# Attention layer: the edge products become the stationary operand of the segment sums, and the denominators go through the output weights

## The chip, the cores and the metric

The kernel runs on one core of a Trainium2 chip. The metric is the device time of one execution in microseconds (us), and the median of several executions is compared. A run's trace holds every instruction of one profiled execution.

## The reference, cut to what matters

Four graph layers follow each other, each with a residual and a layer norm, on 6,250 nodes with 160 features and 100,000 edges sorted by destination. A node's features are 64 scalars and 32 three-vectors. The first layer (L0) is an attention layer, and the change is in it alone. In short:

```
m1 = cg_tp(scalars, vectors of src + dst, edge harmonics, radial weights)   # 96 scalars, 128 three-vectors
a  = exp(score(m1, head) - max over the edges of dst)                       # 4 heads
m2 = cg_tp(gated values of m1, edge harmonics, w2)                          # 96 scalars, 128 three-vectors
val = m2 @ (Ws_vlin, Wv_vlin)                                               # per head 16 scalars, 8 three-vectors
out[dst, head] = sum over edges of a * val / sum over edges of a
```

The value projection is linear, so the kernel sums a*m2 over the edges first and projects the sums per node. One edge's m2 has 480 numbers: three blocks of 128 (the x, y and z parts of the vectors) and one block of 96 scalars. A further column 480 of m2 is a constant 1, whose sum is the softmax denominator.

## The kernel before, in words

The loop of L0 is `edge_loop0`. It takes the edges in windows (`Window0`) of three chunks (`WC = 3`) of 128 edges; 784 chunks make `NW0 = 262` windows. A window owns 32 destination nodes (`WM = 32`), and with 4 heads that gives 128 pairs of head and node. The order of all instructions is written out by hand: in slot `s` of `for s in range(NW0 + 10)`, the windows that entered 1, 2, ... 10 slots ago (`x2` to `x9`, `at(10)`) each do one stage. Every engine runs its instructions in the order in which the slot lists them.

The stages, with the lines of their main instructions:
- `load` gathers the features of the sources (L722, POOL).
- `ends` (L1229) spreads the features of the 32 destinations over the edges by matmuls of 32 rows, `weights` (L1239) makes the radial weights by matmuls of 32 rows.
- `product1` makes m1 on VectorE and GpSimd.
- `turn` transposes one chunk of m1 (four blocks, L1288) and ScalarE copies it out (L1290). `linear` (L1296, L1298) projects it, six passes of 32 columns among them; `gated` and `score` follow.
- `spread`, `scores` (L1330), `exps` and `by_edge` (L1352) make the masked exponentials `p`: edges in the partitions, 128 pairs of head and node in the columns.
- `product2` makes m2 of the window.
- `sums` (L1359): one matmul per chunk with `p` as the stationary operand and the 481 columns of m2 as the moving one. The result `pa` has head and node in the partitions. After the third chunk ScalarE copies it to `a` (L1362).
- `channels`: four transposes of `a` (L1367, L1368) put the 480 channels in the partitions, in four blocks; two copies make `aT` (L1370, L1371).
- `outputs`: one matmul with the 96x64 weights `w["ls"]` (L1377), three with the 128x32 weights `w["lv"]` (L1379). The denominator is copied from column 480 of `a` (L1386), and four copies of 32x40, one per head, fill `row` (L1392 on VectorE, then L1390 three times on ScalarE).
- `write` sends `row` to a table in memory.

A matmul on f32 operands is two passes in the trace, a transpose one; each pass is a load of the stationary operand (LDWEIGHTS, "PEld") and a stream of the moving columns (MATMUL, "PE"). In PSUM the tiles of `ends`, `sums` and `outputs` share one buffer (name `m`, `bufs=1`), so each of them waits until the one before has been read. The transposes of `turn`, `scores`, `by_edge` and `channels` share two buffers (name `t`).

In every fourth slot `radial` loads the harmonics and radial inputs of four windows, and GpSimd multiplies them (L1416). Below, such a slot is called a radial slot.

After the four layers' loops, `Heads` reads the table of L0 and divides by the denominators. Edges that fall outside of their window are handled by a second loop over `Window0`; it does not run on these inputs (L1379 has 1,572 passes, six for each of 262 windows).

## Time and profile before

| | |
|---|---|
| median of 3 runs | 8015.94 us (8013.83 to 8018.99) |
| the profiled execution | 8008.86 us, span 8007.1 us |
| mean granted TensorE clock | 0.948 |
| L0 loop, first L1229 to last L1229 | 306.3 to 3251.0 us |
| L0 loop, 400 to 3250 us: busy PE, DVE, POOL, ACT | 2825, 2294, 2180, 1549 us of 2850 |
| layer 1 loop, 3570 to 5440 us: busy PE, DVE, POOL, ACT | 1870, 1383, 1425, 1084 us of 1870 |
| most slots of the L0 loop | 10.79 us |
| radial slots (every fourth) | 11.55 us |

A slot's length is the distance between successive L1323, of which there is one in each slot. "PEclk" is the clock that TensorE was granted, as a share of the full one; it is 1.0 or 0.5 at any moment, and what lies between is a mean over a stretch. The end of a matmul is modelled in the trace, so a busy PE isn't a PE at its peak: distances from start to start tell what a pass costs.

### The profile page before, as it was taken

How to read it: one execution, taken by the hardware profiler on the slowest of the kernel's cores; microseconds unless marked ns; L12 is line 12 of the kernel's file. 1: busy time of each engine (PE TensorE's matmuls, PEld its weight loads, DVE VectorE, ACT ScalarE, POOL GpSimd, SP SyncE). 2: the span in 40 equal slices, each digit the busy share in tenths (PEclk: the TensorE clock that was granted, in tenths of full speed). 3: DMA queues.
4: the chain of work that ended last, by engine and by line, in shares of the span. 5: the costliest groups of instructions: out<-in, count | busy, mean ns of one | idle time of the engine just before them, and what ended most of it. 6: DMA issues, size and time to landing. Idle time of an engine off the chain costs nothing. (4 is left out here: it accounts for less than half of the span.)

```text
span 8007.1 us, 150406 instructions
## 1 busy us (share of the span) xinstructions
PE 7328.2 (92%) x49240; PEld 5720.5 (71%) x49240; DVE 5391.7 (67%) x11871; ACT 3997.6 (50%) x12138; POOL 5269.2 (66%) x5412
## 2 busy tenths in 40 slices
PE   4899999999999999789999999997888887888887
PEld 2677877787878878569999999995555556555556
DVE  5488888878888788557777777775444446555557
ACT  1255555555555555345555555555555554333334
POOL 0377777777777777117777777772777770677771
PEclk9999999999999999669999999996899998999999
DMA  4344444433333333235565656555333335444446
GB/s 137 99 121 111 112 116 119 109 61 63 60 64 60 64 60 63 53 103 99 100 103 98 100 101 100 98 88 144 87 86 86 86 85 178 112 110 110 110 110 228
DMA packets 645090, 799.53 MB, mean 100 GB/s; under 512 B 185122, under 2 KB 512146, under 8 KB 636722
## 3 DMA queue, kind: packets, MB, share of 16 engines
q1 hardware_dynamic: 404818, 501.89, 22.3%
q0 software_dynamic: 238880, 283.36, 20.5%
q8 instruction: 402, 6.59, 0.4%
q14 instruction: 414, 3.39, 0.1%
q10 hardware_dynamic: 576, 4.30, 0.1%
HBM read 548.48 MB, written 240.64 MB: 99 GB/s over the span
## 5 line engine op out<-in xcount | busy, mean ns | idle before, releaser
L722 POOL DMA_INDIRECT f<-feat,r_src x2352 | 2536.4, 1078 | 969.7 <-issue 550.8
L1081 POOL DMA_INDIRECT tab<-o,scat x784 | 1350.4, 1722 | 433.5 <-ACT o L1080 301.5
L857 PE MATMUL pa<-pr,oy 128*128 128x321 f32 (+1 forms) x3136 | 1110.6, 492 | 0.0
L866 ACT COPY o<-pa 32x96 f32<-32x96 f32 (+4 forms) x2358 | 553.3, 245 | 843.4 <-PE pa L857 797.1
L1067 PE MATMUL pt<-same,tp 128*128 128x128 f32 x6272 | 895.5, 286 | 7.0 <-DVE tp L710 4.0
L857 PEld LDWEIGHTS pa<-pr,oy 128*128 128x128 f32 x3136 | 609.4, 199 | 371.0 <-issue 193.7
L1067 PEld LDWEIGHTS pt<-same,tp 128*128 128x128 f32 x6272 | 764.3, 192 | 24.2 <-PE pf L1051 16.3
L1290 ACT COPY xt<-t 128x512 f32<-128x512 f32 x784 | 460.8, 588 | 592.6 <-PE t L1288 568.7
L1359 PE MATMUL m<-m,p 128*128 128x481 f32 x1568 | 739.0, 581 | 0.9 <-ACT row L1390 0.9
L1069 ACT COPY xt<-pt 128x512 f32<-128x512 f32 x784 | 459.6, 586 | 524.3 <-PE pt L1067 524.3
L1298 PEld LDWEIGHTS z<-w_mv,xt 128*128 128x128 f32 x4704 | 622.1, 195 | 0.0
L1078 PE MATMUL po<-ov,xt 128*128 128x32 f32 x4704 | 611.6, 267 | 0.0
L1323 POOL COPY sc_all<-sc 128x384 f32<-128x384 f32 x262 | 302.8, 1156 | 464.2 <-DVE sc L1318 461.3
L1298 PE MATMUL z<-w_mv,xt 128*128 128x32 f32 x4704 | 601.5, 265 | 0.0
L1078 PEld LDWEIGHTS po<-ov,xt 128*128 128x128 f32 x4704 | 588.3, 192 | 0.0
L807 PE MATMUL ww<-w,hid 64*128 64x192 f32 (+1 forms) x2088 | 260.8, 364 | 297.1 <-DVE pr L839 170.7
L1288 PE MATMUL t<-ident,tp 128*128 128x128 f32 x3136 | 513.9, 288 | 0.0
L1288 PEld LDWEIGHTS t<-ident,tp 128*128 128x128 f32 x3136 | 385.3, 152 | 178.1 <-issue 126.1
L807 PEld LDWEIGHTS ww<-w,hid 64*128 64x128 f32 x2088 | 180.8, 189 | 443.9 <-ACT o L866 208.5
L1303 DVE SCALAR_TENSOR_TENSOR val<-th,z 128x96 f32<-128x96 f32 x784 | 196.3, 250 | 406.6 <-ACT la L1300 406.2
L846 DVE TENSOR_TENSOR pr<-f,ww 128x384 f32<-128x384 f32 x131 | 72.7, 555 | 561.8 <-DMA f<-feat,r_src 255.2
L1299 ACT ACTIVATE th<-z 128x96 f32<-128x96 f32 x784 | 197.0, 251 | 433.9 <-PE z L1298 396.3
(328 smaller groups left out, 16509.6 us busy)
## 6 DMA issues: line engine op xcount, KB each, us to landing
tab<-zeros SPq DMA_DIRECT2D x49, 1280.0 KB
nodes<-in_src_row_dram SPq DMA_DIRECT2D x98, 512.0 KB
dn<-in_dst_row_dram SPq DMA_DIRECT2D x261, 192.0 KB
f<-feat,r_src POOLq DMA_INDIRECT x2352
tb<-tab SPq DMA_DIRECT2D x24, 1280.0 KB
e<-in_ef64T_dram SPq DMA_DIRECT2D x196, 128.0 KB
dn<-in_dst_row_dram SPq DMA_DIRECT2D x196, 128.0 KB
e<-in_ef64T_dram SPq DMA_DIRECT2D x261, 96.0 KB
```

The costliest lines, as they stand in the source:

```text
L722: pool.indirect_dma_start(out=o, out_offset=None, in_=table, in_offset=bass.IndirectOffsetOnAxis(ap=idx, axis=0),)
L807: pe.matmul(self.ww[:, q, 0:wn], self.hid[k, c * P : (c + 1) * P], m, start=True, stop=True)
L857: pe.matmul(pa[:, 0:m], self.oy[:, q, :], self.pr[:, q, 0:m], start=c == 0, stop=c == self.ns[h] - 1)
L866: act.copy(o[q, at : at + e], pa[q, b0 * V : b0 * V + e])
L1067: pe.matmul(pt[:, k, :], self.tp[:, c, lo : lo + P], self.same[:, c, :], start=True, stop=True)
L1069: act.copy(self.xt, pt)
L1078: pe.matmul(po[:, 96 + i * V : 96 + (i + 1) * V], xt[:, 1 + i, :], w["ov"], start=True, stop=True)
L1081: pool.indirect_dma_start(out=self.tables[c % len(self.tables)], out_offset=bass.IndirectOffsetOnAxis(ap=self.scat[:, c : c + 1], axis=0), ...
L1288: pe.transpose(pt[:, k, :], self.tp[:, c, k * P : (k + 1) * P], ident)
L1290: act.copy(self.xt[c], pt)
L1298: pe.matmul(z[:, F + k * V : F + (k + 1) * V], xt[:, k, :], w["mv"], start=True, stop=True)
L1359: pe.matmul(self.pa, self.p[:, c * P : (c + 1) * P], self.m2[:, c, 0:481], start=c == 0, stop=c == self.n - 1)
```

## The change

- `sums` now goes by block `k` of channels. Each block of 128 columns of m2 is the stationary operand and `p` the moving one, so the result has the channels in the partitions and head and node in the columns. There are 12 matmuls of 128 columns in a window where there were three of 481.
- `channels` and its slot are gone, and so is the copy `a`. One copy of 128x512 from `pa` makes `aT`. `outputs` and `write` come one slot earlier (`x8` and `at(9)`), and the loop has one slot fewer.
- Column 480 of m2, the constant 1, is now row 96 of the fourth block of `aT`. The weights `ls` become 97 x 68: per head 16 columns and one more, whose only entry is a 1 in row 96. The matmul with `ls` thus gives the denominator of each pair as well. The copies into `row` take 41 columns, and the copy of the denominator is gone. In `row` and the table the denominator sits at column 16 of 41 instead of 40, and `Heads` reads it there.
- `ls` is set up by two memsets and a strided load.

```diff
-        def sums(self, c):
-            if c == 0:
-                self.pa = self.ps.tile([P, 481], F32, name="m", bufs=1)
-            pe.matmul(self.pa, self.p[:, c * P : (c + 1) * P], self.m2[:, c, 0:481], start=c == 0, stop=c == self.n - 1)
-            if c == self.n - 1:
-                self.a = self.sb.tile([P, 481], F32, name="a", bufs=4)
-                act.copy(self.a, self.pa)
-
-        def channels(self):
-            pt = self.ps.tile([P, 4, P], F32, name="t", bufs=2)
-            for k in range(3):
-                pe.transpose(pt[:, k, :], self.a[:, k * P : (k + 1) * P], ident)
-            pe.transpose(pt[0:96, 3, :], self.a[:, 384:480], ident)
-            self.at_ = self.sb.tile([P, 4, P], F32, name="aT", bufs=2)
-            act.copy(self.at_[:, 0:3, :], pt[:, 0:3, :])
-            act.copy(self.at_[0:96, 3, :], pt[0:96, 3, :])
+        def sums(self, k):
+            if k == 0:
+                self.pa = self.ps.tile([P, 4, P], F32, name="m", bufs=1)
+            q = slice(k * P, (k + 1) * P)
+            for c in range(self.n):
+                pe.matmul(
+                    self.pa[:, k, :], self.m2[:, c, q], self.p[:, c * P : (c + 1) * P], start=c == 0, stop=c == self.n - 1
+                )
+            if k == 3:
+                self.at_ = self.sb.tile([P, 4, P], F32, name="aT", bufs=2)
+                act.copy(self.at_, self.pa)
...
-            pe.matmul(o[:, :, 0:16], self.at_[0:96, 3, :], w["ls"].rearrange("k (h a) -> k h a", h=4), start=True, stop=True)
+            ls = w["ls"].rearrange("k (h a) -> k h a", h=4)
+            pe.matmul(o[:, :, 0:17], self.at_[0:97, 3, :], ls, start=True, stop=True)
...
-            vec.tensor_copy(row[:, 40:41], self.a[:, 480:481])
...
-                    act.copy(row[q, 0:40], o[q, h, :])
+                    act.copy(row[q, 0:41], o[q, h, :])
...
-                for s in range(NW0 + 10):
+                for s in range(NW0 + 9):
...
-                    chunk(x7, 0, "sums")
+                    sums(0)
                     chunk(x4, 1, "turn")
                     x5.exps()
-                    chunk(x7, 1, "sums")
-                    chunk(x7, 2, "sums")
+                    sums(1, 2, 3)
                     on(first, 3)
                     on(second, 3)
                     chunk(x4, 1, "linear", "gated")
                     chunk(x4, 2, "turn")
                     x6.by_edge()
                     x2.masks()
-                    x9.outputs()
+                    x8.outputs()
                     chunk(x4, 2, "linear")
-                    x8.channels()
                     chunk(x4, 2, "gated")
```

More of the change, by code (lines that the diff above doesn't have):

```diff
@@ L523, in begin @@
                 vec.tensor_add(t0[:, :, :, 0:41], t0[:, :, :, 0:41], t1[:, :, :, 0:41])
-                den = t0[:, :, :, 40]
+                den = t0[:, :, :, 16]
                 vec.tensor_scalar(den, den, 1e-16, None, ALU.add)
@@ L531, in begin @@
                 v_ = av[:, 0:m, S:F].rearrange("p j (h a) -> p h j a", h=4)
-                vec.tensor_mul(s_, t0[:, :, :, 0:16], bc(t0[:, :, :, 40], 3, 16))
-                vec.tensor_mul(v_, t0[:, :, :, 16:40], bc(t0[:, :, :, 40], 3, 24))
+                vec.tensor_mul(s_, t0[:, :, :, 0:16], bc(t0[:, :, :, 16], 3, 16))
+                vec.tensor_mul(v_, t0[:, :, :, 17:41], bc(t0[:, :, :, 16], 3, 24))
         def turn(self, i):
@@ L1354, in by_edge @@
             act.copy(self.p[:, 0:e], pt[:, 0:e])
-        def sums(self, c):
-            if c == 0:
-                self.pa = self.ps.tile([P, 481], F32, name="m", bufs=1)
-            pe.matmul(self.pa, self.p[:, c * P : (c + 1) * P], self.m2[:, c, 0:481], start=c == 0, stop=c == self.n - 1)
-            if c == self.n - 1:
-                self.a = self.sb.tile([P, 481], F32, name="a", bufs=4)
-                act.copy(self.a, self.pa)
-        def channels(self):
-            pt = self.ps.tile([P, 4, P], F32, name="t", bufs=2)
-            for k in range(3):
-                pe.transpose(pt[:, k, :], self.a[:, k * P : (k + 1) * P], ident)
-            pe.transpose(pt[0:96, 3, :], self.a[:, 384:480], ident)
-            self.at_ = self.sb.tile([P, 4, P], F32, name="aT", bufs=2)
-            act.copy(self.at_[:, 0:3, :], pt[:, 0:3, :])
-            act.copy(self.at_[0:96, 3, :], pt[0:96, 3, :])
+        def sums(self, k):
[9 more added lines that the diff above has]
+                act.copy(self.at_, self.pa)
         def outputs(self, old=None):
             w, row = self.w, self.row
-            po = self.ps.tile([P, F], F32, name="m", bufs=1)
-            o = po.rearrange("p (h q) -> p h q", q=40)
-            pe.matmul(o[:, :, 0:16], self.at_[0:96, 3, :], w["ls"].rearrange("k (h a) -> k h a", h=4), start=True, stop=True)
+            po = self.ps.tile([P, 4 * 41], F32, name="m", bufs=1)
+            o = po.rearrange("p (h q) -> p h q", q=41)
+            ls = w["ls"].rearrange("k (h a) -> k h a", h=4)
+            pe.matmul(o[:, :, 0:17], self.at_[0:97, 3, :], ls, start=True, stop=True)
             for k in range(3):
                 pe.matmul(
-                    o[:, :, 16 + 8 * k : 24 + 8 * k],
+                    o[:, :, 17 + 8 * k : 25 + 8 * k],
                     self.at_[:, k, :],
@@ L1389, in outputs @@
                 if h:
-                    act.copy(row[q, 0:40], o[q, h, :])
+                    act.copy(row[q, 0:41], o[q, h, :])
                 else:
-                    vec.tensor_copy(row[q, 0:40], o[q, h, :])
+                    vec.tensor_copy(row[q, 0:41], o[q, h, :])
             if old is not None:
@@ L1476, in edge_loop0 @@
                         ws.append(new)
-                    x2, x3, x4, x5, x6, x7, x8, x9 = (at(k) for k in range(2, 10))
+                    x2, x3, x4, x5, x6, x7, x8 = (at(k) for k in range(2, 9))
                     load, first, second = new.load(), x3.product1(), x5.product2()
@@ L1486, in chunk, with sums @@
                             getattr(x, name)(c)
-                    at(10).write(tabs[0][(s - 10) % tab_n[0]])
+                    def sums(*parts):
+                        for k in parts if x7.n else ():
+                            x7.sums(k)
+                    at(9).write(tabs[0][(s - 9) % tab_n[0]])
                     on(load)
@@ L1590, in edge_loop0 @@
                 x.by_edge()
-                for c in range(n):
-                    x.sums(c)
-                x.channels()
+                for k in range(4):
+                    x.sums(k)
                 x.outputs(old)
@@ L1677 @@
             act.copy(ms[:, 128:160], po[0:96, 0, 0:V])
-            ls = load(wp, t["L0_gnn_Ws_vlin"], 96, S, "w_ls")
+            ls = wp.tile([97, 4 * 17], F32, name="w_ls")
+            vec.memset(ls, 0.0)
+            vec.memset(ls[96:97, 16 : 4 * 17 : 17], 1.0)
+            l4 = ls[0:96, :].rearrange("k (h a) -> k h a", h=4)[:, :, 0:16]
+            nc.sync.dma_start(l4, t["L0_gnn_Ws_vlin"].rearrange("k (h a) -> k h a", h=4))
             lv = load(wp, t["L0_gnn_Wv_vlin"], P, V, "w_lv")
@@ L1693 @@
             vec.tensor_scalar(cv[96:P, :], cv[96:P, :], R2, None, ALU.mult)
-            vec.tensor_scalar(ls, ls, cs, 0.5, ALU.mult, ALU.mult)
+            vec.tensor_scalar(l4, l4, cs, 0.5, ALU.mult, ALU.mult)
             vec.tensor_scalar(lv, lv, cv, 0.5, ALU.mult, ALU.mult)
```

## The prediction

> **What bounds the kernel now.** The page's rows of busy time and of the 40 slices come first:

> ```profile
> PE 7328.2 (92%) x49240; PEld 5720.5 (71%) x49240; DVE 5391.7 (67%) x11871; ACT 3997.6 (50%) x12138; POOL 5269.2 (66%) x5412
> PE   4899999999999999789999999997888887888887
> PEclk9999999999999999669999999996899998999999
> ```

> Slices 2 to 15 are the attention loop. PE shows 9 there, no other engine does, and the clock is 9, not full. Two windows of busy time compare that loop with the one of layer 1 (columns after the stretch: busy us and instructions of PE, PEld, DVE, ACT, POOL, then the granted clock):

> ```profile
> 400.00:3250.00 2850.00, 2825.02 (x22778) 2279.61 (x22777) 2294.32 (x5314) 1548.81 (x4810) 2179.79 (x2838) 0.97 0.36 84
> 3570.00:5440.00 1870.00, 1869.60 (x15596) 1710.58 (x15596) 1382.53 (x2096) 1083.57 (x2402) 1425.03 (x866) 1.00 0.59 98
> ```

> TensorE bounds the attention loop: 99% busy, the next engine 80%. So I read its slot as a list of passes. The timeline of PE in a normal slot (start, modelled length, line, shape, passes):

> ```profile
> 571.17 0.60 PE L1288 MATMUL t<-ident,tp 128*128 128x128 f32 x4
> 571.60 1.78 PE L1359 MATMUL m<-m,p 128*128 128x481 f32 x4
> 573.22 0.44 PE L1296 MATMUL z<-w_ms,xt 96*128 96x160 f32 x2
> ...
> 574.88 0.33 PE L1377 MATMUL m<-w_ls,aT 96*128 96x64 f32 x2
> 575.05 0.81 PE L1379 MATMUL m<-w_lv,aT 128*128 128x32 f32 x6
> 575.69 0.52 PE L1296 MATMUL z<-w_ms,xt 96*128 96x160 f32 x2
> 576.05 0.75 PE L1298 MATMUL z<-w_mv,xt 128*128 128x32 f32 x6
> 576.64 0.53 PE L1367 MATMUL t<-ident,a 128*128 128x128 f32 x3
> 577.00 0.27 PE L1368 MATMUL t<-ident,a 128*96 128x128 f32 x1
> 577.20 1.08 PE L1229 MATMUL m<-fw,on 32*128 32x160 f32 x6
> 578.21 0.66 PE L1288 MATMUL t<-ident,tp 128*128 128x128 f32 x4
> ```

> Four passes of sums take 571.60 to 573.22, 0.404 us each. The transposes of `channels` take 576.64 to 577.20. The last view is the clock, by stretches of 3.4 us around one long slot:

> ```profile
> 596.60:600.00 3.40, 2.91 (x24) 2.71 (x24) 2.20 (x9) 2.85 (x12) 2.94 (x5) 1.00 0.20 51
> 600.00:603.40 3.40, 3.40 (x29) 2.74 (x31) 3.19 (x6) 1.55 (x5) 2.36 (x3) 0.50 0.65 64
> 603.40:606.80 3.40, 3.40 (x24) 3.07 (x18) 1.31 (x3) 0.35 (x2) 2.84 (x5) 0.50 0.13 33
> 606.80:610.20 3.40, 3.40 (x8) 1.80 (x8) 3.01 (x8) 0.99 (x2) 2.25 (x4) 0.50 0.09 24
> 610.20:613.60 3.40, 3.40 (x26) 2.78 (x24) 0.65 (x3) 1.89 (x6) 0.96 (x2) 1.00 0.13 30
> ```

> Between 600.0 and 610.2 us TensorE has half its clock, and the slot takes 15.65 us, not 10.79. From 400 us on, the loop has 24 such spells: 13 of 10.2 us, costing 4.86 us each, and 11 of 3.4 us, costing 1.58 us (12.37 for 10.79). Together 81 us.

> [...] every change of clock in this loop lies on one grid of 3.413 us. [...] the trace has 112 ns from load to load (below). [...]

> **The change part by part,** for a full-clock slot:
> - Sums, old: 6 passes x 0.404 = 2.42 us. New: 3 chunks x 4 blocks x 2 passes = 24 passes of 128 columns. Layer 1's L1067 has the same form, both operands in SBUF; eight loads take 0.97 us with the last one's 0.19 in it, so (0.97 - 0.19) / 7 = 0.112 us each:

> ```profile
> 3801.13 0.97 PEld L1067 LDWEIGHTS pt<-same,tp 128*128 128x128 f32 x8
> ```

>   24 x 0.1115 = 2.68 us, **+0.26 us**. Bounds: 0.109 us a pass (the transposes) gives +0.20; 0.114 gives +0.32.
> - `channels` goes: 577.20 - 576.64 = 0.56 us; the step to the 32-row matmuls, 0.206 us for 0.112, moves to the last L1298. **-0.47 us**.
> - `ends` (L1229) now follows the last L1298 directly. It needs PSUM buffer `m`, which the copies into `row` must have read. L1379 ends at 575.86; L1392 and the three L1390 end at 576.70; L1229 could stream at 576.74. Release and load put it at 576.8: a wait of 0 to 0.12 us, taken as **+0.05**. Behind it on PE stand the next `turn` and `weights`.
> - Sum: normal slot 10.79 - 0.16 = **10.63 us**. In radial slots L1377 stands idle about 0.65 us for the copy of the sums (ScalarE is late, behind VectorE, which L1416 slows). The longer sums run into that idle time, so only -0.47 + 0.05 counts: **-0.42**.
> - At full clock: 196 x 0.16 + 66 x 0.42 = 59 us, and 3 us for the drained slot (L1377 to L1377, 2.6 us): **-62 us**.
> - Hidden: ScalarE loses 0.56 + 0.48 + 0.26 and gains 0.59 us, VectorE loses 0.145 (L1386). Both have idle time beside PE. Without that cover they would still have less to do than before. The copies of 41 columns for 40, the 68 columns of `ls` for 64 [...] and `Heads` are the same work: bounds -1 to +1 us. Set-up: two memsets and a load among other loads, 0 to 2 us, taken as 0. No queue gains a DMA in the loop; the table write on SP comes a slot earlier.

> **The clock.** Take the 3.413 us that begin with L1377. Streaming time before: L1377 0.08, L1379 6 x 0.027 = 0.16, L1296 0.20, L1298 0.16, the four transposes 0.43, L1229 6 x 0.133 / 4 = 0.20, a bit of `turn` 0.07; 1.30 / 3.413 = **0.38**, at the limit. After: 0.11 + 0.16 + 0.20 + 0.16 + 0.20 and 0.35 of `turn`; 1.18 / 3.413 = **0.35**, below it. The change takes the densest work out of TensorE's thinnest stretch and turns the sums, which had streaming to spare, into more of it.

> Sliding such a window over four slots, it is below 0.38 in 0.3 us of a normal and 1.24 us of a radial slot before (2.14 us in four), and in 1.05 and 1.38 us after (4.53 us). Spells for phases spread evenly: 4.53 / 3.413 x 65.5 = 87, against 41 for before, which had 24. But the phases aren't even. A spell after the change starts late in the thin stretch, so the first half-clock window can hardly regain the limit (it does 1.8 us of work), and two windows are lost, 3.15 us. A slot is then 13.78 us, 4.04 grid steps, and drifts only 0.13 us against the grid, where an undisturbed one drifts 0.39; a radial slot adds 0.5. Four slots cross 1.0 us of the thin phases, 4.6 slots the rest: 47% of 262, 122 spells. Between 87 and 122 I take 110: 110 x 3.15 = 346 us, for the 81 of before: **+265 us**.

> Total: -62 + 265 = +203 us on the profiled 8009 us. The median of the runs shown stands 7 us above that execution; on it, 8016 + 203 = **8219 us**.

> **The rivals.**
> - The clock doesn't get worse: the limit is a little lower or depends on something else. For: the limit is fitted, and a normal slot lies 0.03 under it; at 0.365, with no wait at L1229, the thin phases all but vanish. Then -62 us, 7954; with no spell left at all -62 - 81 = -143, 7873.
> - Both effects cancel: some 45 spells, 45 x 3.15 = 142 against 81 + 62. About 8016.
> - The loads aren't hidden, since a new stationary operand of m2 comes with each pass. If loads and streams alternated, 0.22 us a pass, 24 x 0.11 = 2.6 us a slot, 690 us: 8700. L1067 speaks against it; it decides from 0.13 us a pass on.
> - The denominators or the copies become the bound: excluded, ScalarE and VectorE lose work.

> **How the numbers follow.** Clock worse: 0.71, own range 8080 to 8400 (65 to 150 spells, some of three windows). Clock not worse: 0.23. Cancelled: 0.04. Exposed loads: 0.02. About 0.2%, 16 us, can be told from no change. The range 7950 to 8390 takes in the gain at an unchanged clock and leaves out its best tail and the worst of the other.

> **What would show it.** Right: clock of the attention loop 0.82 to 0.92; undisturbed normal slots of 10.6 us; three to six times as many long slots, of 13 to 16 us; sums passes 0.112 us apart. Wrong: clock 0.97 or more there, or undisturbed slots not under 10.79 us.

## The result, and the profile after

| | before | after |
|---|---|---|
| median (6 runs each) | 8014.98 us | 8283.94 us |
| ratio, 95% interval | | 1.0334 (1.032 to 1.0347) |
| profiled execution's span | 8007.1 us | 8270.3 us |
| slots of the attention loop, undisturbed: normal, radial | 10.79, 11.55 us | 10.60, 11.57 us |
| spells at half clock in the loop, from 400 us on | 24 | 150 |
| loop, first to last L1323 | 2940.3 us | 3212.1 us |

The clock records in the traces of before and after, 140 and 404 of them, are all 1.0 or 0.5, and each trace's start within 0.02 us of one grid of 3.413 us. A stretch of that grid is a grid window below. A spell is a run of grid windows at half clock, and an undisturbed slot has none in it; the last slots, in which the loop drains, aren't counted. The change makes the kernel slower by 269 us. On the page, PE is as busy as before, and the digits of the clock, counted from 0, fall from 9 to 8 in slices 2 to 15, with one 9 left among them:

```profile
PE 7599.2 (92%) x52896; PEld 6358.0 (77%) x52896; DVE 5367.1 (65%) x11611; ACT 3845.5 (46%) x11614; POOL 5251.3 (63%) x5412
...
PE   4899999999999999978999999997888887898887
...
PEclk9988888888898888857999999998799998999999
```

In the windows of the attention loop and of layer 1 (columns as before: busy us and instructions of PE, PEld, DVE, ACT, POOL, granted clock) the first has 0.86 for 0.97, the second is unchanged:

```profile
400.00:3250.00 2850.00, 2829.59 (x24041) 2654.39 (x24041) 2075.30 (x4622) 1285.49 (x3935) 1992.99 (x2600) 0.86 0.36 79
3870.00:5740.00 1870.00, 1852.92 (x15462) 1696.20 (x15461) 1364.01 (x2075) 1071.72 (x2379) 1415.25 (x861) 1.00 0.58 97
```

The timeline of PE in an undisturbed normal slot:

```profile
1536.30 2.17 PE L1363 MATMUL m<-p,m 128*128 128x128 f32 x18
1538.31 0.44 PE L1296 MATMUL z<-w_ms,xt 96*128 96x160 f32 x2
1538.58 0.75 PE L1298 MATMUL z<-w_mv,xt 128*128 128x32 f32 x6
1539.17 0.64 PE L1288 MATMUL t<-ident,tp 128*128 128x128 f32 x4
1539.64 0.49 PE L1352 MATMUL t<-ident,pT 128*128 128x128 f32 x3
1539.97 0.34 PE L1375 MATMUL m<-w_ls,aT 97*128 97x68 f32 x2
1540.14 0.80 PE L1377 MATMUL m<-w_lv,aT 128*128 128x32 f32 x6
1540.78 0.52 PE L1296 MATMUL z<-w_ms,xt 96*128 96x160 f32 x2
1541.14 0.75 PE L1298 MATMUL z<-w_mv,xt 128*128 128x32 f32 x6
1541.84 1.08 PE L1229 MATMUL m<-fw,on 32*128 32x160 f32 x6
1542.85 0.66 PE L1288 MATMUL t<-ident,tp 128*128 128x128 f32 x4
```

Eighteen passes of the new sums (L1363) take 1536.30 to 1538.31, 0.112 us each. From L1298 to L1229, where the transposes stood, there are now 0.70 us, not 1.15. So the listed work did get shorter: 10.60 us for 10.79. Yet only about a quarter of the slots are that short. The clock around one of the others, by grid windows:

```profile
1503.36:1506.77 3.41, 3.41 (x28) 3.11 (x26) 1.49 (x7) 2.09 (x8) 0.80 (x1) 0.99 0.15 34
1506.77:1510.19 3.42, 3.42 (x32) 2.88 (x30) 3.42 (x5) 1.01 (x2) 2.84 (x2) 0.50 0.33 62
1510.19:1513.60 3.41, 3.41 (x18) 3.41 (x18) 2.42 (x8) 0.35 (x2) 3.13 (x8) 0.51 0.18 44
1513.60:1517.00 3.40, 3.40 (x33) 3.40 (x33) 1.14 (x4) 2.04 (x5) 2.30 (x3) 1.00 0.12 33
```

PE is busy through the whole first window, with 28 passes; but 22 of them are those of L1375, L1377, L1296, L1298 and L1229, most of them with few columns (32) or few rows (32); by the prediction's sum of streaming time its share is 0.37 (its 1.2 columns per ns are the trace's: before's passes of 481 columns take 0.404 us, 1.19 per ns). Two windows at half clock follow, and the slot takes 13.80 us. Of the 150 spells, 120 lie in normal slots: 72 of two windows (3.20 us each, from 13.80 - 10.60), 44 of one (1.57 us, from 12.17 - 10.60) and 4 of three (4.8 us). The other 30 lie in radial slots, where PE waits anyway and they cost less: 24 of two windows (2.28 us, from 13.85 - 11.57) and 6 of one (0.60 us, from 12.17 - 11.57). Together they cost 377 us. The kernel before has 72 us, not the 81 of the prediction: all 11 of its one-window spells lie in radial slots, and cost 12.37 - 11.55 = 0.82 us each, not 1.58.

### The profile page after: what moved, and what is told of

Read it like the earlier page. It is cut to its first block, busy times and chain, and to the rows that moved or that the text cites. A ratio compares the mean times of both kernels' runs of the same rounds, so it can differ in the third digit from the quotient of the medians.

```text
span 8270.3 us, 156617 instructions
## 1 busy us (share of the span) xinstructions
PE 7599.2 (92%) x52896; PEld 6358.0 (77%) x52896; DVE 5367.1 (65%) x11611; ACT 3845.5 (46%) x11614; POOL 5251.3 (63%) x5412
## 5 line engine op out<-in xcount | busy, mean ns | idle before, releaser
L1067 PE MATMUL pt<-same,tp 128*128 128x128 f32 x6272 | 895.3, 286 | 9.9 <-DVE tp L710 6.8
L1363 PE MATMUL m<-p,m 128*128 128x128 f32 x6272 | 872.8, 294 | 1.8 <-ACT row L1387 1.8
L1363 PEld LDWEIGHTS m<-p,m 128*128 128x128 f32 x6272 | 837.7, 212 | 2.0 <-issue 1.0
L1290 ACT COPY xt<-t 128x512 f32<-128x512 f32 x784 | 459.8, 586 | 753.2 <-PE t L1288 726.7
L1067 PEld LDWEIGHTS pt<-same,tp 128*128 128x128 f32 x6272 | 764.2, 192 | 27.0 <-PE pf L1051 16.3
L1323 POOL COPY sc_all<-sc 128x384 f32<-128x384 f32 x262 | 301.5, 1151 | 749.5 <-DVE sc L1318 744.1
L1298 PEld LDWEIGHTS z<-w_mv,xt 128*128 128x128 f32 x4704 | 687.7, 213 | 0.0
L1298 PE MATMUL z<-w_mv,xt 128*128 128x32 f32 x4704 | 653.8, 278 | 0.0
L1288 PE MATMUL t<-ident,tp 128*128 128x128 f32 x3136 | 565.7, 310 | 0.0
L1288 PEld LDWEIGHTS t<-ident,tp 128*128 128x128 f32 x3136 | 417.6, 163 | 45.8 <-issue 45.8
```

The lines of the kernel that those rows point to most:

```text
L1067: pe.matmul(pt[:, k, :], self.tp[:, c, lo : lo + P], self.same[:, c, :], start=True, stop=True)
L1288: pe.transpose(pt[:, k, :], self.tp[:, c, k * P : (k + 1) * P], ident)
L1290: act.copy(self.xt[c], pt)
L1298: pe.matmul(z[:, F + k * V : F + (k + 1) * V], xt[:, k, :], w["mv"], start=True, stop=True)
L1363: pe.matmul(self.pa[:, k, :], self.m2[:, c, q], self.p[:, c * P : (c + 1) * P], start=c == 0, stop=c == self.n - 1)
```

## The experiments

My theory, an estimate fitted to the trace of before: in this loop a grid window whose streaming time, weighted by rows, is below a share of about 0.38 is followed by half clock, and the change takes the four dense transposes out of the thinnest stretch. The rivals: the new passes of the sums cost the time or bring the spells by themselves; PE's busy time or its number of passes tells, and not what they stream; a wait is behind it.

| run | median us | ratio to before (95%) | spells |
|---|---|---|---|
| e1_fill_thin | 8042.46 | 1.0044 (1.0027 to 1.0061) | 16 |
| e2_fill_dense | 8182.81 | 1.0226 (1.0209 to 1.0243) | 122 |
| e3_before_channels_moved | 8073.62 | 1.0091 (1.0075 to 1.0108) | 93 |
| e4_outputs_between | 8939.12 | 1.1162 (1.1143 to 1.118) | 255 |
| e5_after_full_rows | 7874.94 | 0.9848 (0.9828 to 0.9868) | 35 |
| e6_before_full_rows | 7897.71 | 0.9876 (0.9861 to 0.9891) | 27 |
| e7_no_radial_product | 7780.42 | 0.9727 (0.9709 to 0.9744) | 0 |
| e8_split_radial | 7815.53 | 0.9772 (0.9758 to 0.9785) | 0 |
| e9_turn_before_ends | 8525.45 | 0.9599 (0.9551 to 0.9647) | 0 |
| e10_before_full_rows_split | 8565.02 | 0.964 (0.9592 to 0.9689) | 0 |
| e11_after_turn_before_ends | 8718.86 | 0.9829 (0.9762 to 0.9896) | 33 |
| e12_turn_before_ends_again | 8537.27 | 0.9598 (0.9573 to 0.9623) | 0 |

The last four ran on two chips on which the kernel before takes 8882 us (e9, e10, e11) and 8895 us (e12), not 8000. In their traces the loops after layer 1 are longer than on the other chips (in e9 they take 2.9 ms, in e8 2.2 ms); the passes of the attention loop are not. So of these four I compare the attention loops and the medians among each other, not with the others' times or ratios.

**Four transposes back in the thin stretch (e1).** They are ahead of the last `linear`, so one call earlier than where `channels` had stood; the tile `z` grows from 256 to 512 columns for them:

```diff
+            if c == 2:
+                for _ in range(4):
+                    pe.transpose(z[:, 384:512], ident, ident)
```

> The kernel after, with four more 128x128 transposes per window (of the identity, into unused columns of the z bank), in the place where the four transposes of `channels` had stood; nothing reads them. Clock theory (half-clock spells come from the thin stretch between by_edge and turn): the stretch is as dense as before, so the 152 spells fall to 25 to 60; undisturbed normal slots grow by 0.44 us to 11.04; radial slots stay near 11.6. 8270 - 409 for the spells + 86 for the transposes + 80 to 190 for the spells left: a profiled execution of 8030 to 8140 us, faster than after although it does more. Rival (the passes of the sums themselves cost the time): 8270 + 115 = about 8385 us.

Measured: 16 spells, span 8045.6 us, undisturbed normal slots of 10.97 us, 0.37 us more than after's and not the 0.44 expected. Radial slots grew too, to 11.96 us, where I had expected 11.6. The window of the loop from 400 to 3000 us, after and then with the transposes:

```profile
400.00:3000.00 2600.00, 2581.71 (x21963) 2421.75 (x21962) 1896.75 (x4223) 1174.59 (x3595) 1819.98 (x2375) 0.86 0.36 81
```

```profile
400.00:3000.00 2600.00, 2558.94 (x24575) 2414.46 (x24575) 2045.98 (x4550) 1253.64 (x3867) 1980.81 (x2557) 0.98 0.36 86
```

The same 2600 us hold 2,600 passes more. Useless work that lengthens each normal slot by 0.37 us makes the kernel some 230 us faster (ratio 1.0044 for 1.0334). All the new passes of the sums are still there, so they can't be what costs the time.

**The same four transposes in a dense place (e2),** ahead of the ones of `scores`:

```diff
+            if n == 3:
+                for _ in range(4):
+                    pe.transpose(pt[:, 3 * P : 4 * P], ident, ident)
             for c in range(n):
                 pe.transpose(pt[:, c * P : (c + 1) * P], self.sca[:, c, :], ident)
```

> The kernel after, with the same four more transposes per window, but beside `scores`, ahead of the sums, where TensorE streams densely anyway; nothing reads them. Clock theory: the thin stretch is as it was, so 110 to 190 spells stay, and the transposes come on top: 8250 to 8450 us profiled. Rival (any four more transposes raise the activity enough, wherever they stand): as fill_thin, 8030 to 8140 us.

122 spells stay, as expected, so it matters where they stand. The time, 8177 us profiled, is below what I expected: 113 of the 122 are of one window. One-window spells cost 1.57 us in after's normal slots, so by my estimate a window at half clock does 3.41 - 1.57 = 1.84 us of full-rate work. By my theory, whether that reaches the limit depends on where in the slot it falls, and with other slots (11.03 us) it falls elsewhere.

**The kernel before with one call moved (e3):**

```diff
                     x3.weights()
+                    x8.channels()
                     on(second, 2)
...
                     chunk(x4, 2, "linear")
-                    x8.channels()
```

> The kernel before with one call moved: `channels` comes right after `weights` (x3) and no longer after the last `linear`. The same instructions, in another order. Clock theory: the thin stretch is now that of the kernel after, and its spells come: 90 to 180 spells, clock 0.84 to 0.92 in the loop, 8150 to 8380 us profiled, with undisturbed slots still about 10.8 us. Rival (the new form of the sums brings the spells or the time): no change, 8009 within 20 us.

93 spells for 24, clock 0.95, median 67 us over the kernel before of the same chip. So the old sums get the spells as well, once the transposes leave the stretch. The count is in the range, the time below it, and for a reason: all 93 are of one window. `channels` now stands right behind the thin stretch, after `turn` and `weights`, and by my theory the first half-clock window is then dense enough: the 93 of them stream at least 0.39. A normal slot with a spell takes 12.24 us for 10.72, so a spell costs about 1.5 us. The loop is 65 us longer than before's.

**The thin pieces apart (e4):**

```diff
-                    sums(0)
+                    sums(0, 1)
                     chunk(x4, 1, "turn")
+                    sums(2, 3)
                     x5.exps()
-                    sums(1, 2, 3)
...
                     chunk(x4, 1, "linear", "gated")
+                    x8.outputs()
                     chunk(x4, 2, "turn")
                     x6.by_edge()
                     x2.masks()
-                    x8.outputs()
                     chunk(x4, 2, "linear")
```

> The kernel after, reordered: sums of blocks 0 and 1, turn of chunk 1, sums of blocks 2 and 3, exps, linear of chunk 1, `outputs` (x8), turn of chunk 2, by_edge, linear of chunk 2. No instruction more or less; the thin pieces no longer stand together. Clock theory: no stretch of 3.41 us streams less than 0.40 in a normal slot, so under 20 spells are left; undisturbed slots 10.6 us plus 0 to 0.2 us of wait for PSUM buffer m; 8270 - 409 + 0 to 50, so 7860 to 7920 us profiled, faster than the kernel before by 1 to 2%. Rival (the passes of the sums cost the time): about 8270 us.

My expectation failed badly: 255 spells, clock 0.76, 8945 us. The timeline of PE names the cause:

```profile
1518.46 0.63 PE L1288 MATMUL t<-ident,tp 128*128 128x128 f32 x4
1518.93 0.49 PE L1352 MATMUL t<-ident,pT 128*128 128x128 f32 x3
1520.13 0.54 PE L1296 MATMUL z<-w_ms,xt 96*128 96x160 f32 x2 [0.71 <-ACT xt L1290]
1520.51 0.75 PE L1298 MATMUL z<-w_mv,xt 128*128 128x32 f32 x6
1521.19 1.08 PE L1229 MATMUL m<-fw,on 32*128 32x160 f32 x6
```

The last `linear` needs ScalarE's copy of the transposes just made (L1290), and `outputs` had covered that copy. Now PE waits 0.71 us in each slot, in the thin stretch. The wait alone is 0.71 x 262 = 186 us; with the spells the new order costs some 660 us on after (ratio 1.1162 for 1.0334). The order was wrong; the spells are again where PE streams least.

**More rows, no more passes (e5, e6).** The two kernels get the same edit: the tile of destination features has 128 rows, 96 of them zero, so L1229 has the same six passes of 160 columns on 128 rows (shortened; the comment is mine). The rival is that busy time or passes tell, and not rows.

```diff
-            self.fw = sb.tile([WM, F], F32, name="fw", bufs=5)
+            self.fw = next(self.tps[2])    # one of 5 tiles [P, F], zeroed once
...
-            gather(self.fw, feat[1][:, :], self.node_idx)
+            gather(self.fw[0:WM, :], feat[1][:, :], self.node_idx)
...
-                pe.matmul(..., self.on[0:WM, c * P : (c + 1) * P], self.fw, start=True, stop=True)
+                pe.matmul(..., self.on[:, c * P : (c + 1) * P], self.fw, start=True, stop=True)
```

> The kernel after, with `ends` on 128 rows: the features of the 32 destinations lie in a 128-row tile whose other rows are zero, so L1229's passes have 128 rows, not 32, and the same columns. Nothing else changes, and no pass is added. Clock theory, with streaming time weighted by rows: the six passes count 0.80 us, not 0.20, in the thin stretch; its share rises by 0.6 / 3.41 = 0.18 to above 0.5, and the spells all but vanish (under 10). Undisturbed slots 10.4 to 10.6 us (a step between row groups falls away). 8270 - 409 - 0 to 40: 7820 to 7870 us profiled, faster than the kernel before. Rival [...]: about 150 spells stay, 8230 to 8290 us.

> The kernel before with the same edit of `ends`. Clock theory: its 24 spells (81 us) vanish and slots lose 0 to 0.2 us: 8007 - 81 - 0 to 40, 7885 to 7930 us. The distance of after_full_rows to this one is then what the change is worth at an undisturbed clock: 196 normal slots x 0.19 us and nothing in the radial slots, -37 us, -20 to -60 with the bounds; the prediction had -62. Rival (the change costs something else beside the clock): after_full_rows is not faster than this one.

The windows from 400 to 3000 us of e5 and then e6:

```profile
400.00:3000.00 2600.00, 2561.14 (x24705) 2443.00 (x24703) 2117.86 (x4754) 1309.84 (x4037) 2047.45 (x2678) 0.98 0.38 88
```

```profile
400.00:3000.00 2600.00, 2558.13 (x21470) 2130.42 (x21472) 2146.25 (x5011) 1453.60 (x4537) 2054.07 (x2684) 0.98 0.36 88
```

The spells of after fall from 150 to 35, and its ratio to the kernel before from 1.0334 to 0.9848. No pass, column or load was added, so in this loop rows count for the clock, those of zeros included. The spells left sit in radial slots or the slot behind one, where PE also waits (from 400 to 3000 us 49 times for ScalarE's copy ahead of L1375, 37.2 us together). "Under 10" was too few, and the span of 7898 us is above the 7820 to 7870 I gave. Before keeps 27 spells, where I expected none, though 26 of them are of one window. Its 7894 us lie in my range by luck: the slots lost 0.34 us, not 0 to 0.2.

The pair says more. At a clear clock both kernels' normal slots are 10.45 us: the change is worth nothing there. From the last L1298 to L1229 e5 has 0.229 us, where 0.112 would do, and its six passes take 0.92 us, not e6's 0.82. The timelines of PE, e5 and then e6:

```profile
1509.37 0.75 PE L1298 MATMUL z<-w_mv,xt 128*128 128x32 f32 x6
1510.08 1.08 PE L1229 MATMUL m<-fw,on 128*128 128x160 f32 x6
1511.00 0.60 PE L1288 MATMUL t<-ident,tp 128*128 128x128 f32 x4
```

```profile
1511.86 0.27 PE L1368 MATMUL t<-ident,a 128*96 128x128 f32 x1
1511.96 0.98 PE L1229 MATMUL m<-fw,on 128*128 128x160 f32 x6
1512.78 0.38 PE L1288 MATMUL t<-ident,tp 128*128 128x128 f32 x2
```

In e5 L1229 waits for PSUM buffer `m`: its first load starts at 1510.08, 0.05 us after the last copy into `row` has ended (as in after, at 1541.84 for 1541.79). The medians are 23 us apart, e5 the faster, with e5's five runs between 7858 and 7904, while the loop of e5's profile is 8 us the longer one. So at this clock the two are close to equal.

**The radial slots (e7, e8).** After kept them at 11.57 us, where I had expected 0.42 us less. e7 leaves the product out:

```diff
-        pool.tensor_tensor(yr[:, 0:m, :], yr[:, 0:m, :], rb[:, 0:m, :], ALU.mult)
+        pool.tensor_tensor(yr[:, 0:1, 0:8], yr[:, 0:1, 0:8], rb[:, 0:1, 0:8], ALU.mult)
```

> after_full_rows with the radial product left out: GpSimd multiplies a corner of 1x8 columns of `yr`, not 768, every fourth slot, so the radial weights come out without their radial inputs. Theory: radial slots take 11.57 us since L1416 slows VectorE and ScalarE's copy of the sums comes late; without it they are normal slots: 65 x 1.0 = 65 us less than after_full_rows. Rival (the loads of `radial`, or their issue, hold the slot): no change, within 10 us.

> after_full_rows with the radial product in two halves, in the two slots after the one of its loads; same work. If a piece of 0.9 us fits into the slack of a slot (the copy of the sums has 0.3 to 0.9 us), all slots are near 10.5 us and it gains 30 to 65 us on after_full_rows; if a piece costs as much per us as the whole, no change.

e8 issues `yr[:, 0:3]` one slot after the loads and `yr[:, 3:6]` two slots after them. Without the product all slots are 10.45 us, PE is never idle and no spell is left:

```profile
400.00:3000.00 2600.00, 2600.00 (x25858) 2499.92 (x25857) 2127.65 (x4975) 1374.46 (x4231) 2062.49 (x2800) 1.00 0.38 91
```

That is 95 us less than e5 in the medians, 120 in the spans (7778.0 for 7898.3), of which 65 x 1.12 = 73 are the slots. I put the other 47 down to the 35 spells, which I had not counted. In halves, the two slots with a piece take 10.75 us each and the others 10.45: 59 us less than e5, 0.9772 of before. Of the kernels that do the whole computation it is the fastest on the chips of the first eight runs.

**Turn before ends (e9, e10, e11, e12).** The same line moves in e8 (e9, e12) and in after (e11); e10 is before with the edits of e8.

```diff
-                    x3.ends()
                     on(second)
                     chunk(x4, 0, "turn")
+                    x3.ends()
```

> split_radial with `ends` (x3) one place later, after the turn of chunk 0: the same instructions. In split_radial L1229 starts 0.12 us later than its passes allow and its six passes take 0.92 us, not the 0.82 of before_full_rows, so it waits about 0.2 us for PSUM buffer m (the copies into `row`). With four transposes in between, 0.44 us, that wait is gone: slots of 10.2 to 10.3 us for 10.45, 40 to 55 us less than split_radial, no spells. Rival (VectorE or GpSimd has become the bound of these slots): no change, within 10 us.

> The kernel before with both edits of split_radial: `ends` on 128 rows and the radial product in two halves. Theory: no spells, slots 10.45 and 10.75 us as in split_radial, since what the change gains on passes it loses in the wait for m; 7815 to 7850 us, within 30 us of split_radial. Rival (the change is worth its 37 us or more at an undisturbed clock): 7850 us or more.

> The kernel after with only that one call moved: `ends` after the turn of chunk 0, still on 32 rows. Clock theory: the four transposes stand between the last `linear` and `ends`, the lowest share in a normal slot is about 0.385 for 0.344, so spells come from radial slots alone, 10 to 60 of them; one step between row groups falls away, slots 10.4 to 10.5 us; 7860 to 7990 us, faster than the kernel before. Rival: 8270 us, or 150 spells.

> turn_before_ends once more, beside the kernel before on the chip of this call, since the chip of its first run took 10% longer for every kernel in the later layers. The slots of the attention loop were 10.27 us without and 10.76 us with a piece of the radial product, against 10.45 and 10.76 in split_radial: half of 262 slots x 0.18 = 24 us less than split_radial. Theory: ratio to the kernel before 0.974, that is 7780 to 7800 us for 8000; no spells in the loop. Rival (the loop's gain is lost later): ratio as split_radial, 0.977.

e9: slots without a piece 10.27 us, with a piece 10.76, so the wait was there (0.18 us), and in the slots with a piece the rival holds: they don't gain. The loop is 2748 us (2751 in the repetition), e8's 2767: 16 to 19 us, not the 40 to 55 of the first expectation. The repetition came to another chip with the same long later loops, so its 7780 to 7800 us stays untested. e10: no spells, slots of mostly 10.1 to 10.9 us with a mean of 10.67 (e8: 10.60), loop 2786 us, 19 more than e8. Against e9 it is 38 us longer in the loop and 40 us in the median of the same chip: with its wait covered, the changed kernel is 40 us ahead. How much the same move would give the kernel before was not tried, so not all of the 40 us need be the change's. e11: one moved line takes after's spells from 150 to 33 and its loop from 3212 to 2932 us, below the 2940 of before; its slots are 10.25 us, under the 10.4 I gave, and it is faster than before on its chip (ratio 0.9829, up to 0.9896).

## Why the prediction was right, and where it was off

It gave 8219 us, slower, for 8284; 203 us for 269. By its steps:
- **TensorE bounds the loop; a pass costs 0.112 us.** Right: the loads of 16 passes of L1363 in one stretch of the trace take 1.87 us, (1.87 - 0.19) / 15 = 0.112.

```profile
1536.41 1.87 PEld L1363 LDWEIGHTS m<-p,m 128*128 128x128 f32 x16
```

- **Normal slot 10.63 us.** 10.60 measured. L1229's wait was put at 0.05: from L1298 it starts 0.228 us later, for 0.206 expected, 0.02 us. The step from passes of 128 rows to those of 32 (0.206 us in before, for 0.10 from L1368 to L1229 in e6, where both have 128) hid the rest: in e5 there is no such step, and L1229 still starts 0.229 us after L1298.
- **Radial slots, -0.42 us.** This term was mis-sized: they went from 11.55 to 11.57, so nothing was gained and 66 x 0.42 = 28 us of the predicted gain were missing. I took the end of the idle time before L1377 as fixed against the slot's start, and counted what follows as gain. The timeline of a radial slot of after, with what leads to L1375:

```profile
1544.89 1.81 POOL L1413 TENSOR_TENSOR yr<-yr,rb 128x768 f32<-128x768 f32 x1
1545.04 2.58 DVE L1273 TENSOR_TENSOR x<-val,r_y 128x864 f32<-128x864 f32 x1
...
1550.30 0.61 ACT L1343 ACTIVATE pT<-s,neg 128x384 f32<-128x384 f32 x1 [2.62 <-DVE neg L1341]
...
1550.82 0.57 ACT L1368 COPY aT<-m 128x512 f32<-128x512 f32 x1
...
1551.44 0.44 PE L1375 MATMUL m<-w_ls,aT 97*128 97x68 f32 x2 [0.71 <-ACT aT L1368]
```

  While GpSimd multiplies, VectorE's L1273 takes 2.58 us, not the 1.05 of most slots (the line at the end of this point is before's, with the shortest, median and longest in ns), and everything behind it is late, up to ScalarE's copy. The slot is VectorE's, and a PE that is done sooner waits longer (0.87 us for 0.65). e7 and e8 show it: L1273 takes 1.05 us in every slot of e7 and 1.8 us beside each half of the product in e8, and the slots follow. e2 agrees, with 0.4 us more of PE ahead of that wait and radial slots still of 11.57 us. Why e1's four transposes, behind the wait, lengthen them to 11.96 us I haven't traced.

```profile
L1273 DVE TENSOR_TENSOR x<-val,r_y x262: 451/1052/2580, 330.9 to 3270.2; 128x864 f32<-128x864 f32 x131
```

- **110 spells of 3.15 us, +265.** The cause was right: e1 takes the spells from 150 to 16 with the new sums in place, e3 from 24 to 93 without them, e5 from 150 to 35 with rows alone. The sizes were off: 150 spells (6.3 times before's 24, just past the "three to six times"), at a mean price of 377 / 150 = 2.51 us. That the total, 346 us, comes near 377 is in part luck: too few spells at too high a price. Two-window spells in normal slots cost 3.20 us, for 3.15 predicted; that the first half-clock window could hardly regain the limit failed for 50 of 150, and the 30 in radial slots cost less. The same slip is in the 81 us for the kernel before, which are 72. A small one is in the share of the thin stretch: L1375's streaming is 2 x 68 / 1.2 x 97 / 128 = 86 ns, not 0.11 us, which makes 0.34 of the 0.35.
- **The limit near 0.38.** In before, after and e1 to e4 together, from 400 us to the end of the loop, 4,375 grid windows are at full clock, 665 of them ahead of a spell. One limit fitted to the streaming share, 0.381, puts 4 of them on the wrong side. With rows left out of the weight the best limit misplaces 380, with transposes left out 408; by PE's busy time it is 451, and by the number of passes 666, no better than no limit at all. In before and after alone, with 174 windows ahead of a spell and 1,270 others, 0.381 misplaces 2, without rows it is 90, without transposes 169, by busy time or passes 174. With e5, e6 and e11 added, 0.381 misplaces 30 of 6,671 windows, so the limit is near, not sharp. After a half-clock window the clock returns from a share of about 0.37 on, counted in full-rate work (36 of 1,106 misplaced).
- **The sum.** Loop: 377 - 72 = +305 for spells, -37 for 196 normal slots, +1 for radial ones, makes +269; measured +272. Outside of the loop -9, which I haven't traced. Together +263 on the profiled execution.

That rows count comes from the fit (380 windows misplaced without them, for 4) and e5 (spells from 150 to 35). That these f32 transposes count comes from the fit and e1, where four more of them took the spells from 150 to 16. What sets the clock beyond this fit, no run shows.

## What to carry to other kernels

Where TensorE bounds a stage and its clock isn't full, cost an edit twice: the passes it adds or removes, and what it does to the stretch in which TensorE streams least, here over 3.413 us. Keep dense passes between thin ones (e1: spells from 150 to 16), fill rows that are free (e5: from 150 to 35), and look before moving a piece at which copy it was covering (e4: 0.71 us of wait in each slot). Here a zero-padded operand gave back more than the change had lost. It also took 100 us from the kernel before, so the two padded kernels are only 23 us apart.

## What the runs showed of the hardware that I had not expected

- Half clock can follow a window in which PE is 100% busy: 127 of after's 150 windows ahead of a spell are at least 99% busy, but by rows and columns they stream only 0.34 to 0.38 of the time.
- Rows of zeros count for the clock of this loop: with 96 of them under the same six passes, after's spells fall from 150 to 35.
- Four transposes of the identity, which lengthen a normal slot by 0.37 us, save some 230 us net. An order that puts a wait of 0.71 us into the thin stretch of each slot costs some 660 us.
- VectorE's L1273 goes from 1.05 to 2.58 us while GpSimd's L1413 runs.
